# Channel sums of the nodes by way of DRAM instead of TensorE transposes, in a two-layer graph network

## The chip, the cores and the metric

The kernel runs on one core of one Trainium2 chip. The metric is the device time of one execution in microseconds (us). Three runs of the kernel before gave 2660.5 to 2662.49 us, with a median of 2661.98 us.

A core has engines with instruction streams of their own: TensorE (PE in the profile) multiplies matrices, VectorE (DVE) and ScalarE (ACT) work on elements, GpSimd (POOL) does small element work and issues DMAs, and the sync engine (SP) issues most DMAs. Each stream runs in its order; an instruction that waits for a semaphore holds back what stands behind it in its stream.

## What is computed

There are 16 graphs (B) with 1024 nodes (N) and 256 channels (C), all in float32. Both layers take relu(layernorm(x)) and add their output to x. The first layer, cut to what matters:

```python
fea = jnp.transpose(x, (0, 2, 1))            # x here is relu(layernorm(x))
c_adj = jnp.mean(fea, axis=1)                # one number for each node
diff = c_adj[:, None, :] - c_adj[:, :, None]
A = jnp.abs(jnp.abs(jax.nn.sigmoid(diff) - 0.5) - 0.5) * 2.0
Wg = adj[None, :, :] * (A + jnp.transpose(A, (0, 2, 1))) * 0.5
g = jax.nn.relu(jnp.einsum('bcn,bnm->bcm', fea, Wg) * para.reshape(1, C, N))
# q from g (4 heads of 64), k and v from x @ kv_w
attn = jax.nn.softmax(jnp.einsum('bhnd,bhmd->bhnm', q, k) * scale, axis=-1)
out = jnp.einsum('bhnm,bhmd->bhnd', attn, v)
```

The second layer multiplies by the normalized adjacency matrix, and then by two weight matrices with a batch norm after each.

The matrix A holds, for each pair of nodes, a function of the difference of their channel sums. To build 128 rows of it, the kernel needs the sums of those 128 nodes as a column (one on each partition), and the sums of all 1024 nodes as a row that is the same on every partition. The change is about how that row is made.

## The kernel before

*Layout.* A node tile has 128 nodes on the partitions; a graph has 8 of them. `Norm` computes a graph's layer norm. Its `relu` on ScalarE also sums the channels of each node into `csum`, a tile of 128 x 8: element [p, t] is the sum for node 128 t + p. That is the column form.

*The row form.* `columns_of` copies the 8 columns on VectorE, each spread over 128 elements, into two tiles `cb` of 128 x 512. `broadcast_row` transposes each of the 8 blocks of 128 x 128 on TensorE (line 199), and ScalarE copies the two PSUM banks to the tile `cbc` (line 200). `cbc` is 128 x 1024: on each partition the sums of all nodes. `differences` makes `cbc` and the generator `weigh`. The same two helpers serve the row of the degrees (`dbc`), once.

*Who reads it.* `weigh` makes the weighted matrix in 8 tiles `w`. For each, ScalarE takes two `Abs` of `cbc` with the column as bias (line 421) and a `Tanh` (line 429), and VectorE multiplies by a tile of adj (line 408) that SP has loaded (line 170).

*Order of the work.* The program order is written by hand. `attention` goes through the graphs in 16 steps each. A step issues the scores of two key tiles (line 858) and their exponentials on ScalarE (line 866), then the products with the values of the step before (line 899), and then background work until a budget is used up: `total` (lines 972 and 973) is spread evenly over the 16 steps of a graph, and each background piece yields its cost, which is added to `done`. Most pieces are products that cost 1.71.

A piece that yields `TOP` ends the step's background; what comes after it is issued in the next step right after the scores, ahead of the products with the values.

*Background of graph b* (from 1 to 13): keys and values of graph b + 1 and its queries, whose left part is the weigher's result (4 + 14 + 4 products); the second layer's `aggregate` of graph b - 1 (14 products), along which `Norm` of graph b + 2 runs; and then `prepare(b + 2, ...)`. This makes the row of graph b + 2, begins its weigher, and transposes h (`transposed`, line 379), along the 8 products of `hidden(b - 1)`, whose results ScalarE copies out as y (line 708). The products go to two PSUM banks in turn (`bank`), which `broadcast_row` and `transposed` use too. In `prepare`, one product stands ahead of `TOP` and the row, and the weigher begins after the second product.

Graph 0's row is made ahead of the attention, graph 1's at the beginning of graph 0's background, graph 2's at its end. Graphs 14 and 15 have no `prepare`, as there is no further graph.

`shifted=True` is a second version of the whole program, behind a branch that these inputs don't take.

Of the kernel before, what the change touches and what calls it, by code (L numbers as in the profile page):

```python
# [10 lines left out]
F32 = mybir.dt.float32  # L11
# [6 lines left out]
P = 128  # L18
# [5 lines left out]
def gnn_two_layers_kernel(  # L24
# [12 lines left out]
    nc = tc.nc  # L37
    B, N, C = x.shape
# [14 lines left out]
    dram = ctx.enter_context(tc.tile_pool(name="dram", bufs=1, space=DRAM))  # L53
# [15 lines left out]
    aht_d = dram.tile([7, NP // 2, P, TH, FB], F32, name="aht_d")  # L69
    y1_d = [dram.tile([P, HC, FB], F32, name=f"y1_d{i}") for i in range(B * NH)]  # L70

    sums_d = [dram.tile([2, FB], F32, name=f"sums_d{u}") for u in range(B * CC * NH)]

    UNITS = B * CC * NH
# [9 lines left out]
    def layers(shifted):  # L84
# [109 lines left out]
        def broadcast_row(dst, cbs, name):  # L194

            for g, cb in enumerate(cbs):
                pt = bank(f"cbp_{name}_{g}")
                for j in range(4):
                    nc.tensor.transpose(pt[:, j * P : (j + 1) * P], cb[:, j, :], ident)
                nc.scalar.copy(dst[:, g * FB : (g + 1) * FB], pt)  # L200
# [165 lines left out]
        TOP = -1.0  # L366
# [14 lines left out]
                    )  # L381
                nc.vector.tensor_copy(ht[:, g * FB : (g + 1) * FB], pt)

        def differences(b, cbs):

            cbcs[b] = p1.tile([P, N], F32, tag="cbc", name=f"cbc_{b}")
            broadcast_row(cbcs[b], cbs, f"c{b}")
            weighers[b] = weigh(b)

        def weigh(b):  # L390


            csum, cbc = csums[b], cbcs[b]
            made = weighted[b] = []
            adjs = []

            def load():
                q, th = divmod(len(adjs), NP)
                adjs.append(load_adj(q, th, f"adj_{b}_{q}_{th}"))

            load()
            for slot in range(2 * NH * NP + 1):
                i, odd = divmod(slot, 2)
                q, th = divmod(i, NP)
                if not odd and i > 0:

                    w, a = made[i - 1], adjs[i - 1]
                    nc.vector.scalar_tensor_tensor(w, w, 1.0, a, op0=ALU.add, op1=ALU.mult)  # L408
                    if b == 0:
                        q, th = divmod(i - 1, NP)  # L410
                        nc.vector.tensor_reduce(
                            rows[:, q, th * TH : (th + 1) * TH], a, AX.X, ALU.add
                        )
                if not odd and i < NH * NP:
                    q, th = divmod(i, NP)
                    if i + 1 < NH * NP:
                        load()
                    w = p8.tile([P, TH, FB], F32, tag="w", name=f"w_{b}_{q}_{th}")
                    made.append(w)
                    for t in range(TH):  # L420
                        nc.scalar.activation(  # L421
                            w[:, t, :],
                            cbc[:, q * FB : (q + 1) * FB],
                            AF.Abs,
                            bias=csum[:, th * TH + t : th * TH + t + 1],
                            scale=-1.0,
                        )
                if odd:
                    nc.scalar.activation(made[i], made[i], AF.Tanh, scale=-0.5 / C)  # L429
                yield 0.0  # L430
# [307 lines left out]
        def prepare(b, products):  # L738


            cbs = columns_of(csums[b], f"c{b}")
            yield from islice(products, 1)
            yield TOP
            differences(b, cbs)
            yield 1.0
            w = weighers[b]
            for k in range(CC):
                yield from weave(islice(products, 3), (0, islice(w, AHEAD // 2)))
                yield TOP
                transposed(b, k)  # L750
                yield 1.0
            yield from products
# [3 lines left out]
        def background(b):  # L756

            if b == 0:
                differences_1 = columns_of(csums[1], "c1")
                yield TOP  # L760
                differences(1, differences_1)
                yield 1.0
                for k in range(CC):
                    yield TOP
                    transposed(1, k)
                    yield 1.0
                w, products, norm = weighers[1], keys_values(1), Norm(2, True).all()
                yield from weave(
                    islice(products, 4), (0, double(islice(w, 8))), (0, islice(norm, 4))
                )  # L770
                yield from weave(
                    plain_queries(1), (0, norm), (0, w), (5, graph()), (7, degrees())
                )
                load_later()
                yield from islice(products, 1)
                cbs = columns_of(dinv, "deg")
                yield from islice(products, 1)
                yield TOP
                broadcast_row(later["dbc"], cbs, "deg")
                yield 1.0  # L780
                yield from prepare(2, products)
                return
            before = hidden(b - 1)
            gather = aggregate(b - 1)
            if b + 1 < B:
                w, products, norm = weighers[b + 1], keys_values(b + 1), normed(b - 1)
                yield from weave(islice(products, 4), (0, islice(w, 4)))
                yield from weave(queries(b + 1), (0, double(w)), (9, islice(norm, 5)))
                yield next(gather)
                yield from weave(products, (0, norm))  # L790
            else:
                yield from weave(endings.pop(), (2, normed(b - 1)))
                yield next(gather)
            if b + 2 < B:
                yield from weave(gather, (7, Norm(b + 2, True).all()))
                yield from prepare(b + 2, before)
            elif b + 2 == B:

                yield from gather
                endings.append(before)  # L800
            else:
                yield from gather
                yield from weave(before, (0, normed_last()))
# [206 lines left out]
        with st:  # L1010
            if shifted:
                for b in range(B):
                    if b > 0:
                        load_x(b)
                    run(Norm(b, True).all())
                    differences(b, columns_of(csums[b], f"c{b}"))
                    for k in range(CC):
                        transposed(b, k)
                    run(islice(weighers[b], AHEAD))
                    run(weave(plain_queries(b), (0, weighers[b])))  # L1020
                    if b == 0:
                        run(degrees(), graph())
                        load_later()
                        broadcast_row(later["dbc"], columns_of(dinv, "deg"), "deg")
                    run(keys_values(b))
                    shifted_attention(b)
                    norm = Norm(b, False)
                    run(norm.all())
                    nc.gpsimd.dma_start(out=x1_d[b], in_=xs[b])
                    if b == B - 1:  # L1030
                        attn.close()
                        turns.append(second(kind))
                    run(aggregate(b), hidden(b))
            else:
                norm = Norm(0, True)
                norm.stats(0, 1)
                norm.scale(0, 2)
                for t in range(2, NT, 2):
                    norm.stats(t, t + 1)
                    norm.shift(t - 2, 2)  # L1040
                    norm.relu(t - 2, t - 1)
                    norm.scale(t, 2)
                norm.shift(NT - 2, 2)
                norm.relu(NT - 2, NT - 1)
                products = keys_values(0)

                for k in range(CC):
                    transposed(0, k, (0,))
                run(islice(products, 2))
                for k in range(CC):  # L1050
                    transposed(0, k, (1,))
                differences(0, columns_of(csums[0], "c0"))
                run(weave(products, (0, islice(weighers[0], AHEAD))))
                load_x(1)
                load_x(2)
                run(weave(plain_queries(0), (0, weighers[0]), (5, Norm(1, True).all())))
                attention()
                attn.close()
                turns.append(second(kind))
                run(aggregate(B - 1), hidden(B - 1))  # L1060
# [324 lines left out]
```

## Time and profile before

| what | value |
|---|---|
| time, median of three | 2661.98 us |
| span of the profiled execution | 2658.7 us |
| granted TensorE clock, mean | 0.988 of full speed |
| PE busy | 2572.0 us, 97% |
| DVE busy | 1743.4 us, 66% |
| ACT busy | 1336.5 us, 50% |
| POOL busy | 564.0 us, 21% |
| transposes of line 199 for `cbc` | 128, of which 120 for graphs 1 to 15 |
| SP waiting in the adj loads of line 170 for VectorE's line 408 | 896.0 us in 71 waits |

In the views of groups, a line gives the engine, the operation, output and input tiles with their shapes, how many there are, and their durations. The timeline lists start, duration, engine and line in order of time. `SPq` is the sync engine's stream: there the duration of a merged line covers the waits between its DMAs. "DMA to landing" is the time from the issue of a transfer until its semaphore says that it is complete. A transfer that was issued behind others on the same queue includes their time.

### The profile page before, as it was taken

The numbers are of one execution on the slowest core, as the hardware profiler recorded it, in microseconds if no ns is written. First come the engines' busy times: TensorE is split into PE (matmuls) and PEld (weight loads), VectorE is DVE, ScalarE is ACT, GpSimd is POOL, SyncE is SP. The second block draws the span as 40 slices with busy tenths as digits, with TensorE's granted clock in tenths as the row PEclk, the third lists the DMA queues.
The fourth block names the chain that finished last, engine by engine and source line by source line (L and its number), as shares of the span: only waits on it lengthen the run. The fifth ranks groups of instructions, "written<-read, shape, count | busy, mean of one in ns | idle before, by whom it ended". The sixth has DMA issues, their size and how long they took to land. (4 is left out here: it accounts for less than half of the span.)

```text
span 2658.7 us, 32181 instructions
## 1 busy us (share of the span) xinstructions
PE 2572.0 (97%) x11882; PEld 951.8 (36%) x11882; DVE 1743.4 (66%) x2768; ACT 1336.5 (50%) x1937; POOL 564.0 (21%) x648
## 2 busy tenths in 40 slices
PE   8959999999999999999999999999999999999995
PEld 3323333333333333333333333333333333334443
DVE  5537576666767675767666676757676675557675
ACT  5635463636454554546373645545463634335544
POOL 1461111111111111111111111111101111026653
PEclk9989999999999999999999999999999999999997
DMA  4451424242423324242424233231524232455559
GB/s 159 145 181 61 166 80 171 84 171 80 143 92 117 122 68 158 68 171 84 171 80 156 87 131 103 93 139 60 174 80 171 80 124 99 135 198 198 198 181 374
DMA packets 131686, 355.59 MB, mean 134 GB/s; under 512 B 17984, under 2 KB 34880, under 8 KB 125376
## 3 DMA queue, kind: packets, MB, share of 16 engines
q1 hardware_dynamic: 104768, 274.25, 29.4%
q0 software_dynamic: 26752, 79.20, 9.0%
q8 instruction: 96, 1.57, 0.2%
q14 instruction: 70, 0.57, 0.1%
HBM read 278.67 MB, written 74.71 MB: 133 GB/s over the span
## 5 line engine op out<-in xcount | busy, mean ns | idle before, releaser
L866 ACT ACTIVATE p<-sc 128x1024 f32<-128x1024 f32 x512 | 495.5, 1019 | 606.3 <-PE sc L858 605.2
L888 DVE TENSOR_TENSOR acc<-acc,p 128x1024 f32<-128x1024 f32 x384 | 471.7, 1228 | 132.0 <-ACT p L866 111.5
L858 PE MATMUL sc<-q,k 64*128 64x512 f32 x2048 | 508.8, 615 | 0.5 <-ACT p L866 0.5
L899 PE MATMUL o<-p,v 128*64 128x512 f32 x2048 | 496.7, 606 | 0.0
L158 PE MATMUL pg<-w,h_a 128*64 128x512 f32 x1600 | 358.1, 592 | 3.4 <-ACT k L595 1.7
L158 PE MATMUL pa<-aht,h_b 128*64 128x512 f32 x1536 | 343.5, 592 | 0.0
L858 PEld LDWEIGHTS sc<-q,k 64*128 64x128 f32 x2048 | 176.1, 186 | 320.4 <-issue 296.8
L919 POOL DMA_DIRECT2D sums_d<-row x64 | 37.5, 586 | 1032.0 <-ACT row L918 1032.0
L158 PE MATMUL py<-at,w 128*64 128x512 f32 x1024 | 230.4, 592 | 0.0
L899 PEld LDWEIGHTS o<-p,v 128*64 128x64 f32 x2048 | 124.5, 136 | 285.4 <-issue 284.7
L408 DVE SCALAR_TENSOR_TENSOR w<-w,adj 128x1024 f32<-128x1024 f32 x128 | 157.2, 1228 | 102.9 <-ACT w L429 99.1
L158 PEld LDWEIGHTS pg<-w,h_a 128*64 128x64 f32 x1600 | 115.5, 137 | 231.8 <-issue 212.8
L158 PEld LDWEIGHTS pa<-aht,h_b 128*64 128x64 f32 x1536 | 110.4, 137 | 213.3 <-issue 197.6
L708 ACT ACTIVATE y<-py,vec 128x512 f32<-128x512 f32 x128 | 87.6, 684 | 168.2 <-PE py L158 111.4
L421 ACT ACTIVATE w<-cbc,csum 128x512 f32<-128x512 f32 x256 | 170.0, 715 | 0.0
L885 DVE TENSOR_TENSOR acc<-p,p 128x1024 f32<-128x1024 f32 x64 | 78.4, 1226 | 109.5 <-ACT p L866 109.5
L709 POOL DMA_DIRECT2D y_d<-y x128 | 70.0, 547 | 316.7 <-ACT y L708 315.6
L429 ACT ACTIVATE w<-w 128x1024 f32<-128x1024 f32 x128 | 134.9, 1054 | 1.8
L483 DVE TENSOR_TENSOR w<-w,w 128x1024 f32<-128x1024 f32 x112 | 132.8, 1216 | 1.8 <-DVE w L408 0.5
L158 PE MATMUL pv<-kvw_f,ht 128*64 128x256 f32 x1024 | 121.0, 384 | 8.8 <-DVE q L575 5.2
L924 POOL DMA_DIRECT2D inv<-sums_d x128 | 98.2, 771 | 145.8 <-DMA sums_d<-row 109.6
L158 PEld LDWEIGHTS py<-at,w 128*64 128x64 f32 x1024 | 74.2, 137 | 145.2 <-issue 128.7
(155 smaller groups left out, 2868.8 us busy)
## 6 DMA issues: line engine op xcount, KB each, us to landing
aht<-aht_d SPq DMA_DIRECT2D x224, 512.0 KB, 6.2
adj<-in_adj_dram SPq DMA_DIRECT2D x128, 512.0 KB, 4.3
y_d<-y POOLq DMA_DIRECT2D x128, 256.0 KB, 2.6
yin_f<-y_d SPq DMA_DIRECT2D x32, 1024.0 KB, 6.3
x<-in_x_dram SPq DMA_DIRECT2D x32, 512.0 KB, 5.0
para<-in_para_dram SPq DMA_DIRECT2D x64, 256.0 KB, 3.9
x_d<-x POOLq DMA_DIRECT2D x16, 1024.0 KB, 10.3
xo_f<-x_d SPq DMA_DIRECT2D x32, 512.0 KB, 8.3
```

The source lines that it names most:

```text
L158: nc.tensor.matmul(dst[r], left[:, r], right, start=start, stop=stop)
L408: nc.vector.scalar_tensor_tensor(w, w, 1.0, a, op0=ALU.add, op1=ALU.mult)
L421: nc.scalar.activation(w[:, t, :], cbc[:, q * FB : (q + 1) * FB], AF.Abs, bias=csum[:, th * TH + t : th * TH + t + 1], scale=-1.0,)
L429: nc.scalar.activation(made[i], made[i], AF.Tanh, scale=-0.5 / C)
L483: nc.vector.tensor_sub(block(i)[part], block(x)[part], block(y)[part])
L708: nc.scalar.activation(y, made, AF.Identity, bias=b1[:, j : j + 1])
L858: nc.tensor.matmul(sc[:, e, :], ks[b][k][r, m * P : (m + 1) * P], qs[b][k][r, f * FB : (f + 1) * FB], start=True, stop=True,)
L866: nc.scalar.activation(pr, sc, AF.Exp)
L885: nc.vector.tensor_add(self.acc, self.held, pr)
L888: nc.vector.tensor_add(self.acc, self.acc, pr)
L899: nc.tensor.matmul(self.o[r, :], vs[b][k][:, m, r], pr[:, e, :], start=(m == 0), stop=(m == NT - 1),)
L924: nc.gpsimd.dma_start(out=self.inv[:, :, e], in_=sums_d[u][e].rearrange("(j q) -> q j", q=P))
```

## The change

For all graphs but the first, the row no longer goes through VectorE, TensorE and ScalarE. SP writes `csum` to a DRAM row `csum_d[b]` of 1024 numbers, transposed by its addresses, and then reads this row back with a partition step of 0, so that `cbc` gets it on all 128 partitions. The second DMA waits for the first. It is meant to take the transposes from TensorE. `differences` makes the columns itself where it still needs them (graph 0). `prepare` calls it at its beginning, without a `TOP` of its own, and now two products stand ahead of the weave with the weigher, so that the weigher begins after the third product.

```diff
+    csum_d = [dram.tile([N], F32, name=f"csum_d{b}") for b in range(B)]
...
-        def differences(b, cbs):
+        def differences(b):
             cbcs[b] = p1.tile([P, N], F32, tag="cbc", name=f"cbc_{b}")
-            broadcast_row(cbcs[b], cbs, f"c{b}")
             weighers[b] = weigh(b)
+            if b == 0:
+                broadcast_row(cbcs[b], columns_of(csums[b], f"c{b}"), f"c{b}")
+                return
+            nc.sync.dma_start(out=csum_d[b].rearrange("(t p) -> p t", p=P), in_=csums[b])
+            nc.sync.dma_start(
+                out=cbcs[b], in_=csum_d[b].rearrange("(o n) -> o n", o=1).to_broadcast([P, N])
+            )
...
         def prepare(b, products):
-            cbs = columns_of(csums[b], f"c{b}")
-            yield from islice(products, 1)
-            yield TOP
-            differences(b, cbs)
-            yield 1.0
+            differences(b)
+            yield from islice(products, 2)
             w = weighers[b]
             for k in range(CC):
                 yield from weave(islice(products, 3), (0, islice(w, AHEAD // 2)))
...
             if b == 0:
-                differences_1 = columns_of(csums[1], "c1")
-                yield TOP
-                differences(1, differences_1)
-                yield 1.0
+                differences(1)
                 for k in range(CC):
                     yield TOP
                     transposed(1, k)
...
-                differences(0, columns_of(csums[0], "c0"))
+                differences(0)
                 run(weave(products, (0, islice(weighers[0], AHEAD))))
```

The calls in the shifted version change in the same way.

More of the change, by code (lines that the diff above doesn't have):

```diff
@@ L1015, in layers @@
                     run(Norm(b, True).all())
-                    differences(b, columns_of(csums[b], f"c{b}"))
+                    differences(b)
                     for k in range(CC):
```

## The prediction

> **What bounds the kernel now.** I read the page first, then the busy time by stretches, then the tile views of the row that is replaced, then the timeline of one graph's end, engine by engine.
>
> ```profile
> PE 2572.0 (97%) x11882; PEld 951.8 (36%) x11882; DVE 1743.4 (66%) x2768; ACT 1336.5 (50%) x1937; POOL 564.0 (21%) x648
> ```
>
> ```profile
> L199 PE MATMUL cbp_c<-ident,cb_c x128: 272/273/329, 18.4 to 2070.8; 128*128 128x128 f32 x128
> L200 ACT COPY cbc<-cbp_c x32: 580/592/616, 19.0 to 2071.6; 128x512 f32<-128x512 f32 x32
> ...
> 762.03:907.28 145.25, 145.05 (x699) 51.88 (x697) 98.28 (x156) 74.12 (x110) 22.10 (x30) 1.00 0.35 117
> ```
>
> The three are the page's busy times, the tile view of the row's transposes and copies (minimum, median and maximum ns) and a stretch. TensorE (PE) is busy 97% of the span. The stretch (its length, then busy us of PE, PE's weight loads, DVE, ACT and POOL, clock, DMA share, GB/s), one whole graph in the steady part (start to start of the transposes of two graphs), says it better: 145.05 us of PE in 145.25 us. So in the middle of the kernel each PE microsecond taken away is a microsecond won, and each stall put in is lost. VectorE at 98.28 us and ScalarE (ACT) at 74.12 us have room, if their work comes in time. The chain of waits covers only the end (from 2386.93 us on), and shows nothing of this change.
>
> The edge that matters is the end of a graph. PE there:
>
> ```profile
> 757.43 1.03 PE L916 MATMUL sums<-acc,ones 128*64 128x512 f32 x4
> 758.29 1.89 PE L158 MATMUL py<-at,w 128*64 128x512 f32 x8
> 760.11 1.99 PE L858 MATMUL sc<-q,k 64*128 64x512 f32 x8
> 762.02 1.09 PE L199 MATMUL cbp_c<-ident,cb_c 128*128 128x128 f32 x8
> 763.05 1.94 PE L899 MATMUL o<-p,v 128*64 128x512 f32 x8
> 764.81 5.32 PE L158 MATMUL py<-at,w 128*64 128x512 f32 x24
> 770.06 1.99 PE L858 MATMUL sc<-q,k 64*128 64x512 f32 x8
> ```
>
> and ScalarE and the sync queue (SP):
>
> ```profile
> 760.08 0.19 ACT L324 ACTIVATION_READ_ACCUMULATOR h_a<-x,lnsm_a 128x1 f32 x1
> 767.38 1.32 ACT L421 ACTIVATE w<-cbc,csum 128x512 f32<-128x512 f32 x2
> ```
>
> ```profile
> 732.34 60.55 SPq L170 DMA_DIRECT2D adj<-in_adj_dram  x6
> ```
>
> The channel sums are complete at 760.27 us, and the row `cbc` is first read at 767.38: 7.1 us. SP runs ahead: at 732.34 it had begun the adj loads of the next weigher.
>
> **What the Trainium skill says.** "TensorE: Matmul & The Clock Gate", Part 4, gives about 275 ns for one 128x128 transpose in a kernel. The trace agrees (273 ns), but they overlap: eight take 1.09 us, 136 ns each. "DMA: Bandwidth & Descriptors", Rules for kernel authors, says that a strided last dimension becomes one descriptor per element: the new write is 1024 elements of four bytes, 64 for each of 16 engines; its section Bandwidth puts such a packet at about 10.5 ns, so I estimate 0.7 us of moving. The same page (Two DMAs through the same engine are not ordered) says that the reader of what a DMA wrote has to wait on its semaphore; the two transfers are therefore a serial chain. The trace has such a pair: the `inv` gathers wait for the write to `sums_d`.
>
> **The change, part by part.**
>
> *Removed.* For 15 of 16 graphs eight transposes, two ACT copies of 0.59 us and two DVE copies of 0.42 us. On PE 15 x 1.09 = 16.4 us. ACT and DVE are not the bound; I count their 1.1 and 0.8 us per graph as nothing, hidden beside PE.
>
> *Added.* A write of 4 KB and a broadcast read of 512 KB per graph, on SP. 15 x 0.5 MB is 2% more traffic, nothing at a DMA share of 0.35. What counts is latency. For the write, the nearest rows are:
>
> ```profile
> L924 POOL DMA_DIRECT2D inv<-sums_d x128: 747/774/805, 100.7 to 2337.3; - x128
> DMA to landing us min/median/max: 2.5/2.6/5.6
> ```
>
> ```profile
> L60 SPq DMA_DIRECT2D vec<-in_vecs_dram x1: 391/391/391, 0.7 to 0.7; - x1
> DMA to landing us min/median/max: 1.6/1.6/1.6
> ```
>
> `inv` moves 512 four-byte elements in 2.6 us, `vec` 9 KB of short rows in 1.6 us. Twice as many elements as `inv`, but without GpSimd's 0.77 us of issue: bounds 2.0 and 3.5, I take 2.7. The read has the shape of an `aht` load (128 rows of 4 KB, same queue):
>
> ```profile
> L628 SPq DMA_DIRECT2D aht<-aht_d x224: 319/324/1216, 263.5 to 2354.7; - x112
> DMA to landing us min/median/max: 3.0/6.2/13.5
> ```
>
> 3.0 us alone; the median has other loads ahead in the queue, which this read doesn't have, as SP waits for the write just before it. Against it run the y stores of 256 KB. Bounds 3.0 and 7 (all 128 rows read the same 4 KB of DRAM, which no load here does); I take 3.6. With 0.2 us for two releases: 0.2 + 2.7 + 3.6 = 6.5 us (bounds 5.2 and 10.7). The row is there at 760.27 + 6.5 = 766.8.
>
> *Moved.* The budget of a step is (37.6 + 24 + 6 + 13.7) / 16 = 5.08 (lines 972 and 973), a product costs 1.71. Before `prepare` 4 + 14 + 4 + 14 products have cost 61.56. In step 12 (due 66.06) the kernel before makes one product, meets TOP and breaks; the new one makes three (66.69). So PE has, from 758.29: three products to about 763.5, scores of step 13 to 765.4, values to 767.2, two products to 770.7, scores of step 14. The first read of `cbc` on ACT stands behind the third product's y (done 764.2): ACT is there at 764.2 and waits until 766.8, some 2.6 us, 13 times (graphs 3 to 15; for graphs 1 and 2 the sums are long done).
>
> *Who is behind that wait.* On ACT: two abs (1.32), both exps of step 13 (1.94), y, tanh (1.05), y. With L the landing, exps end at L + 3.3, the two y at L + 3.95 and L + 5.7. On PE: the scores of step 14 at 770.7 need the first exp (L + 2.3) and 771.7 the second: L up to 768.3. The transposes of h at 773.2 and 773.7, behind 1.9 of scores and 0.6 of `ot`, need the two y's banks: L up to 768.0. Values of step 13 need exps at 774: not binding. So PE stalls only if the row lands after 768.0, if the chain takes over 7.7 us. My 6.5 leaves 1.2 us. On SP, behind the wait for the sums: the adj loads that now start at 732 go out after the row, about 764, and land by 769 (one 512 KB load moves in 1.7 us); the first is used behind a tanh that ends at about 771.8. Hidden beside ACT's work.
>
> *End of the graph.* Step 14 now makes three products and reaches 76.24 of a due 76.22, so step 15 has no background, and the second group of h transposes comes at the change of graph. The exps of step 15 end about 785.0 by the same count, the next scores start about 785.8: no stall. In graph 0 the removed TOP takes one of three thin attention steps away (PE waits of 0.45 and 0.47 us at 62.4 to 65.4); worth at most 1 us, not counted.
>
> Sum: 2662.0 - 16.4 = 2645.6 us.
>
> **The rivals.**
> 1. The chain is longer than the slack: the wait goes from ACT over to PE. For: two DRAM round trips, gaps of 7.1 us now, and `sums_d` to `inv` already cost POOL up to 7.3 us once. At 9.5 us the stall is 1.8 us x 13 = 23.4, less 16.4: 2669. At the upper bound of 10.7 it is 3.0 x 13 = 39, so 2684.6. Against: the queue is empty when the two go out, and quiet landings of all shapes here are 1.6 to 3.6 us.
> 2. The row lands in time, but the new order of pieces (an empty step 15, ACT's work late by 2.6 us, DVE's copies of h behind a late w) opens about 1 us per graph at PE: 13 to 16 us, which takes the gain back: 2660. For: the margins counted above are 0.8 to 1.2 us. Against: each is positive, and scores and exps are double buffered.
> 3. More is won than the transposes, as PE's first steps lose their waits and ACT and DVE are freer: 16.4 + 3 gives 2642. PE's 0.2 us of idle per graph leaves little for it.
>
> **How the numbers follow.** The forecast 0.60, rival 1 0.25 (slower in nearly all of it), rival 2 0.10 (mostly within 0.2%, 5.3 us), rival 3 0.05. So faster by over 0.2%: 0.60 + 0.05 + 0.01 = 0.66, the same 0.10, slower 0.24. The range begins at 2640, below rival 3, and reaches to 2678, a chain of 10.2 us (stall 2.5 x 13 = 32.5, less 16.4), which leaves the slow broadcast outside.
>
> **What would show it.** Right: transposes of `cbc` only in graph 0; ACT waiting some 2.6 us for the row's DMA, 13 times; the write landing near 2.7 us and the read near 3.6; a period of 144.2 us instead of 145.25, with PE busy in all but 0.2 us of it; adj loads going out after the row. Wrong: PE waiting in scores for an exp, or in h's transposes for a y, each graph; a landing after 768.0 on this clock; the period above 145.25. The step on which all hangs is the sum 2.7 + 3.6 against 7.7.

## The result and the profile after

The changed kernel takes 2772.6 us in the median (2771.43 to 2773.67), against 2661.24 us for the kernel before beside it: a ratio of 1.0418 with a 95% interval of 1.04 to 1.0436. It is 111 us slower, where 16 us less was forecast. The range given ended at 2678.

First the page of the kernel before, one line that now matters: the scores, with the number of matmuls, busy us, mean ns, and the idle time ahead of them with its releaser.

```profile
L858 PE MATMUL sc<-q,k 64*128 64x512 f32 x2048 | 508.8, 615 | 0.5 <-ACT p L866 0.5
```

The page of the kernel after (its lines of code are numbered differently: 860 is 858 before, 868 is 866, 429 is 421):

```profile
PE 2585.4 (93%) x11762; PEld 948.4 (34%) x11762; DVE 1728.3 (62%) x2738; ACT 1320.4 (48%) x1907; POOL 560.0 (20%) x648
...
L860 PE MATMUL sc<-q,k 64*128 64x512 f32 x2048 | 534.3, 642 | 105.4 <-ACT p L868 105.4
...
L429 ACT ACTIVATE w<-cbc,csum 128x512 f32<-128x512 f32 x256 | 170.4, 717 | 154.5 <-DMA cbc<-csum_d 154.5
```

TensorE (PE) was busy 97% and is busy 93%. ScalarE (ACT) now waits 154.5 us for the row's DMA, and TensorE 105.4 us for exponentials, where it waited 0.5. The scores are 25.5 us longer in sum, though they are as many as before. The loss can be read off one edge of a graph. The sync engine's timeline (start, duration; the second DMA waits for the first):

```profile
940.27 0.37 SPq L393 DMA_DIRECT2D csum_d<-csum  x1
950.93 0.32 SPq L394 DMA_DIRECT2D cbc<-csum_d  x1
```

ScalarE in the same stretch:

```profile
943.64 0.69 ACT L716 ACTIVATE y<-py,vec 128x512 f32<-128x512 f32 x1 [1.03 <-PE py L159]
956.27 1.33 ACT L429 ACTIVATE w<-cbc,csum 128x512 f32<-128x512 f32 x2 [11.95 <-DMA cbc<-csum_d]
957.51 1.91 ACT L868 ACTIVATE p<-sc 128x1024 f32<-128x1024 f32 x2
```

and TensorE:

```profile
947.20 3.60 PE L159 MATMUL py<-at,w 128*64 128x512 f32 x16
958.57 3.78 PE L860 MATMUL sc<-q,k 64*128 64x512 f32 x8 [7.76 <-ACT p L868]
```

The write is issued 0.03 us after the last sum. The read can only go out 10.66 us later. The row is first used at 956.27, 16.0 us after the write. The two exponentials of that step stand behind it on ScalarE. TensorE does the work that it still has, up to 950.8, and then waits 7.76 us for the first of them. And what follows is slow: eight matmuls of the scores take 3.78 us instead of 1.99. Why, the busy time by stretches shows (stretch, length, busy us of PE, PE's weight loads, DVE, ACT and POOL with the instructions, the granted clock, the share of the DMA engines, GB/s):

```profile
943.00:951.00 8.00, 7.81 (x36) 2.32 (x32) 0.33 (x1) 0.69 (x1) 1.78 (x4) 1.00 0.91 79
951.00:958.00 7.00, 0.00 (x0) 0.00 (x0) 0.00 (x0) 1.73 (x3) 0.00 (x0) 0.81 0.78 233
958.00:960.00 2.00, 1.44 (x4) 0.84 (x6) 1.35 (x2) 2.00 (x4) 0.00 (x0) 0.50 0.83 320
960.00:962.00 2.00, 2.00 (x6) 0.34 (x2) 2.00 (x3) 2.00 (x4) 0.72 (x2) 0.50 0.30 119
...
786.56:940.27 153.71, 146.01 (x690) 51.64 (x688) 96.99 (x154) 73.05 (x108) 22.40 (x29) 0.98 0.37 114
```

After the pause the granted clock is 0.50 for the scores. The same happens at the row of each graph from 3 to 15: 13 waits of 7.2 to 8.5 us, each with eight scores of 3.5 to 3.8 us behind it. The last line is a whole graph: 153.71 us, where it was 145.25. In the sum of this graph 7.76 of waiting, 1.79 of slow scores and 1.03 of saved transposes (see the second experiment) give +8.5 us, and 13 such graphs +111 us.

### The profile page after: what moved, and what is told of

The parts are those of the page before. It is cut to its first block, busy times and chain, and to the rows that moved or that the text cites. A ratio compares the mean times of both kernels' runs of the same rounds, so it can differ in the third digit from the quotient of the medians.

```text
span 2770.7 us, 31886 instructions
## 1 busy us (share of the span) xinstructions
PE 2585.4 (93%) x11762; PEld 948.4 (34%) x11762; DVE 1728.3 (62%) x2738; ACT 1320.4 (48%) x1907; POOL 560.0 (20%) x648
## 3 DMA queue, kind: packets, MB, share of 16 engines
q0 software_dynamic: 26752, 79.20, 11.3%
## 5 line engine op out<-in xcount | busy, mean ns | idle before, releaser
L860 PE MATMUL sc<-q,k 64*128 64x512 f32 x2048 | 534.3, 642 | 105.4 <-ACT p L868 105.4
L860 PEld LDWEIGHTS sc<-q,k 64*128 64x128 f32 x2048 | 183.4, 193 | 426.6 <-issue 279.5
L429 ACT ACTIVATE w<-cbc,csum 128x512 f32<-128x512 f32 x256 | 170.4, 717 | 154.5 <-DMA cbc<-csum_d 154.5
```

The costliest lines, as they stand in the source:

```text
L429: nc.scalar.activation(w[:, t, :], cbc[:, q * FB : (q + 1) * FB], AF.Abs, bias=csum[:, th * TH + t : th * TH + t + 1], scale=-1.0,)
L860: nc.tensor.matmul(sc[:, e, :], ks[b][k][r, m * P : (m + 1) * P], qs[b][k][r, f * FB : (f + 1) * FB], start=True, stop=True,)
```

## The experiments

All edits are against the changed kernel. Experiments 4, 8 and 12 compute what the kernel before computes. The others are made for timing alone: 1 leaves the row in another order, and the rest take it from another tensor, so that their weights are not those of the reference. "Landing" is the time from the issue of a transfer to its completion (minimum, median, maximum of 15).

**1. The same sums, written in rows of 32 bytes.**

```diff
-nc.sync.dma_start(out=csum_d[b].rearrange("(t p) -> p t", p=P), in_=csums[b])
+nc.sync.dma_start(out=csum_d[b].rearrange("(p t) -> p t", p=P), in_=csums[b])
```

> The changed kernel, but the sums are written to DRAM as they lie: 32 contiguous bytes from each partition instead of eight separate four-byte elements. The row comes out in another order (node 8p+t in the place of 128t+p), so the adjacency weights belong to wrong pairs; all work, sizes and waits are the same. Theory A (four-byte pieces in DRAM are slow to complete): the write completes in about 2.2 us instead of 8.5 to 11, the chain of both transfers takes 6 to 7.5 us, ScalarE waits 2 to 3.5 us for the row and TensorE not at all; about 2645 us, near the forecast. Rival B (any DRAM round trip at this point takes this long, whatever the pieces): the write stays above 7 us, about 2760 us or more.

Measured: 2641.23 us, a ratio of 0.992 (0.9903 to 0.9937). The sync engine's timeline:

```profile
752.57 0.32 SPq L393 DMA_DIRECT2D csum_d<-csum  x1
753.98 0.32 SPq L394 DMA_DIRECT2D cbc<-csum_d  x1
754.35 1.70 SPq L171 DMA_DIRECT2D adj<-in_adj_dram  x3
```

ScalarE:

```profile
758.85 1.33 ACT L429 ACTIVATE w<-cbc,csum 128x512 f32<-128x512 f32 x2 [2.23 <-DMA cbc<-csum_d]
```

and one graph by stretches:

```profile
608.35:752.58 144.23, 144.03 (x690) 51.02 (x688) 97.27 (x154) 73.31 (x108) 22.45 (x29) 1.00 0.37 121
```

The write is over in 1.41 us instead of 10.66, the chain takes 6.28, and TensorE runs through. The same 4 KB go the same way through DRAM: rival B falls. What took the time is the form of the write.

**2. No write, the row read from another tensor.**

```diff
-nc.sync.dma_start(out=csum_d[b].rearrange("(t p) -> p t", p=P), in_=csums[b])
...
-    out=cbcs[b], in_=csum_d[b].rearrange("(o n) -> o n", o=1).to_broadcast([P, N])
+    out=cbcs[b], in_=para[0:1, :].to_broadcast([P, N])
```

> The changed kernel without the write of the sums; the row is read from the first row of para instead, in the same broadcast and at the same place, so there is no chain and the weights are computed from another row. It shows what the removed transposes and the new order of pieces are worth without the latency. Theory A: 2643 to 2647 us, 16 below before, a period of about 144.2 us. Rival C (the new order of pieces itself leaves TensorE waiting): 2655 us or more. Under rival B the same as under A.

Measured: 2644.69 us, a ratio of 0.9933 (0.9917 to 0.995). One graph, by stretches:

```profile
583.59:727.81 144.22, 144.02 (x692) 51.01 (x688) 97.31 (x155) 73.16 (x107) 22.42 (x29) 1.00 0.37 121
```

1.03 us less than before, with TensorE idle for 0.2 us as before. So in the steady part the removed transposes are worth nearly what the timeline of the kernel before said (1.09), and the new order of the pieces costs nothing: rival C falls.

**3. The slow write kept, but nothing waits for it.** The write as in the change, the read from `para` as in experiment 2.

> The changed kernel with the slow write of four-byte elements kept, but with the row read from the first row of para (weights from another row), so that nothing waits for the write. If the loss is the wait alone (theory A): as without the write, within 3 us, 2643 to 2649 us. Rival D (the write slows the transfers beside it, the read of the row and the y stores above all): 10 us or more above the run without the write, with the read landing after 5 us or more.

Measured: 2757.58 us, a ratio of 1.0355 (1.0338 to 1.0372), nearly as slow as the change. The tile view of the row in this run, its read and how long it took to land:

```profile
L394 SPq DMA_DIRECT2D cbc<-in_para_dram x15: 566/572/574, 57.6 to 2159.7; - x15
...
DMA to landing us min/median/max: 12.1/12.6/15.0
```

and the tile view of the written row:

```profile
L393 SPq DMA_DIRECT2D csum_d<-csum x15: 370/370/462, 57.1 to 2159.3; - x15
...
DMA to landing us min/median/max: 9.9/12.1/12.6
```

The read is issued 0.4 us after the write and has no semaphore to wait for, but in all 15 cases it completes after the write, by 0.4 to 5.4 us; without the write it landed after 5.3 us (experiment 2). My theory that the loss was the dependence alone fell here: a slow write holds up the transfer behind it too. Rival D had this right.

It is not only the write's own queue. The trace of the change shows the same on GpSimd's, in the `inv` gathers (2.5, 2.6 and 5.6 us to landing in the kernel before):

```profile
L926 POOL DMA_DIRECT2D inv<-sums_d x128: 747/772/805, 99.7 to 2449.9; - x128
...
DMA to landing us min/median/max: 2.5/3.5/10.1
```

In graphs 3 to 15, 26 of them are issued while the write is under way, when the read of the row has not yet gone out. Their packets are over 2.7 to 6.9 us before the write completes, but all 26 complete only 0.2 to 2.6 us after it, 5.9 to 10.1 us after their issue.

**4. The weigher later, the transfers unchanged.**

```diff
-            yield from islice(products, 2)
-            w = weighers[b]
-            for k in range(CC):
-                yield from weave(islice(products, 3), (0, islice(w, AHEAD // 2)))
-                yield TOP
-                transposed(b, k)
-                yield 1.0
+            yield from islice(products, 5)
+            yield TOP
+            transposed(b, 0)
+            yield 1.0
+            yield from weave(islice(products, 3), (0, islice(weighers[b], AHEAD // 2)))
+            yield TOP
+            transposed(b, 1)
+            yield 1.0
...
-                yield from weave(islice(products, 4), (0, islice(w, 4)))
+                yield from weave(islice(products, 4), (0, double(islice(w, 6))))
```

> The changed kernel with the same two transfers, but the weigher begins two steps later: five products of hidden ahead of the first transposes of h, three weigher slots beside the last three products, and the slots that are left over taken two at a time in the next graph's keys (six instead of four). The chain stays as slow as it is (8.5 to 11 and 5.5 us), but it ends about when ScalarE first needs the row. Theory A: the wait of ScalarE falls from 12 us to 0 to 3, TensorE no longer waits for exps; 2645 to 2652 us. Rival C: the order costs, above 2662 us. Rival D: above 2660 us, as the stores beside the write still are slow.

Measured: 2652.99 us, a ratio of 0.9963 (0.9949 to 0.9977), just above the span that theory A gave, and better than the kernel before. One graph by stretches:

```profile
1196.58:1340.80 144.22, 144.03 (x690) 51.05 (x688) 97.42 (x154) 72.97 (x108) 22.45 (x29) 1.00 0.41 121
```

The row is still 16 to 18 us on its way, and here nobody waits for it. In the steady part the period is that of experiment 2 in most graphs, and at most 0.65 us longer (the graph after this one took 144.73), about 2 us in all. The larger part of the distance to experiment 2 lies in the first graphs: TensorE's wait in the degrees' transposes for VectorE's v copies, 4.5 us without the write, is 10.8 us here. Which transfer is held up there was not followed.

**5, 6, 7. What is slow in the write.** All with the unlinked read of experiment 3, so that only the write differs:

```diff
# 5: 64 bytes from element to element
-csum_d = [dram.tile([N], F32, name=f"csum_d{b}") for b in range(B)]
+csum_d = [dram.tile([N, 16], F32, name=f"csum_d{b}") for b in range(B)]
-nc.sync.dma_start(out=csum_d[b].rearrange("(t p) -> p t", p=P), in_=csums[b])
+nc.sync.dma_start(out=csum_d[b][:, 0].rearrange("(t p) -> p t", p=P), in_=csums[b])
# 6: half of the elements
+nc.sync.dma_start(out=csum_d[b][: N // 2].rearrange("(t p) -> p t", p=P), in_=csums[b][:, : NT // 2])
# 7: from GpSimd
+nc.gpsimd.dma_start(out=csum_d[b].rearrange("(t p) -> p t", p=P), in_=csums[b])
```

> The run with the unlinked read (row from para, weights from another row), with each of the 1024 four-byte elements written 64 bytes from the next instead of 4. As many pieces of the same size, but none in the neighbourhood of another. Theory A1 (pieces that fall into the same stretch of memory hold each other up): the write lands in 2 to 5 us instead of 12, and the time falls from 2757 to 2645 to 2665 us. Rival A2 (every small write costs its own time, wherever it goes): the write lands after 10 to 13 us as before, 2750 to 2765 us.

> The run with the unlinked read (row from para, weights from another row), with half of the elements written: the first four columns, 512 elements of four bytes, and the other half of the sums left out. If the completion grows with the number of pieces (A1 and A2 alike), the write lands after 5.5 to 7 us instead of 12 and the row comes some 5 to 6 us earlier: 2665 to 2700 us. If there is a fixed time for a write of short pieces, whatever their number (rival A3), it lands after 11 to 12.5 us, at about 2755 us.

> The run with the unlinked read (row from para, weights from another row), with the write of four-byte elements issued by GpSimd instead of SP, so that it lies in another queue than the read of the row. If the memory is what is slow (theory A): the write lands after 9 us or more from this queue too, and the read beside it, though not behind it in a queue, still takes over 5 us; 2680 to 2760 us. If it is the sync engine's queue, which serves the read only after the write (rival E): the read lands in 3 to 5 us and the time is 2645 to 2660 us.

The tile view of `csum_d` for the spread elements (2644.15 us, ratio 0.9933, 0.9913 to 0.9953):

```profile
L393 SPq DMA_DIRECT2D csum_d<-csum x15: 370/371/501, 58.0 to 2054.1; - x15
...
DMA to landing us min/median/max: 2.8/3.1/5.6
```

for half of the elements (2660.19 us, ratio 0.9993, 0.9984 to 1.0002):

```profile
L393 SPq DMA_DIRECT2D csum_d<-csum x15: 370/371/488, 53.9 to 2058.9; - x15
...
DMA to landing us min/median/max: 10.1/10.5/13.0
```

and from GpSimd (2684.23 us, ratio 1.0084, 1.0064 to 1.0104):

```profile
L393 POOL DMA_DIRECT2D csum_d<-csum x15: 899/902/1121, 57.4 to 2089.3; - x15
...
DMA to landing us min/median/max: 9.4/11.3/12.5
```

As many four-byte pieces, 64 bytes apart, land in 3.1 us instead of 12.1: rival A2 falls, and it is the neighbourhood that counts. Half as many pieces, as dense as before, still need 10.5 us: the number counts for little. A3 came nearest in this, though below its 11 to 12.5 us, and its fixed time for every write of short pieces doesn't fit the 3.1 us of the spread elements. The time of the half write says little and lies in no forecast, since this write needs only the first four node tiles' sums and goes out some 10 us earlier. From the other queue the write is as slow: it is not the sync engine's queue. The run from GpSimd didn't answer the other half of its question, as the read, no longer behind a wait for the sums, went out long before the write; the gathers under experiment 3 answer it, against rival E. What this run lost is another thing, in TensorE's waits:

```profile
PE htp L380 <- ACT y L716: 24.5, 8, 3.9
```

The y stores stand behind the write on GpSimd's queue, so their buffers come free late, and ScalarE's y and TensorE's banks after them: in this trace ScalarE's y waits 44.3 us for the y stores, in nine waits, and not at all in experiment 2.

**9, 10, 11. How dense is too dense.** As in 5, with other distances, and in 11 with each partition's elements in a stretch of its own:

```diff
# 9: [N, 2], 8 bytes apart; 10: [N, 4], 16 bytes apart
+nc.sync.dma_start(out=csum_d[b][:, 0].rearrange("(t p) -> p t", p=P), in_=csums[b])
# 11: [N, 2], 8 bytes apart, a partition's eight elements next to each other
+nc.sync.dma_start(out=csum_d[b][:, 0].rearrange("(p t) -> p t", p=P), in_=csums[b])
```

> The run with the unlinked read (row from para, weights from another row), the 1024 four-byte elements written 8 bytes apart, half as dense as in the change. The two ends are known: 4 bytes apart lands after 12.1 us in the median, 64 bytes apart after 3.1. If writes into one stretch of memory go one after another (theory A1), so that the time goes with how many share a stretch: about 3.1 + 9 x 7/15 = 7.3 us (6 to 8.5). If only direct neighbours disturb each other (rival A4), so that any gap is enough: 3 to 4 us.

> The same with the elements 16 bytes apart. Theory A1: 3.1 + 9 x 3/15 = 4.9 us to landing (4.2 to 6). Rival A4: 3 to 4 us.

> The run with the unlinked read (row from para, weights from another row), elements 8 bytes apart, but in the order of the partitions: the eight elements of one partition lie in one stretch of 64 bytes, and no other partition writes there. As dense as the run with 8 bytes[...]. If it is several engines at once that hold each other up (A5): 3 to 4 us to landing. If it is the number of writes to a stretch, whoever sends them (A1): as with 8 bytes, 6 to 8.5 us.

One execution each. The landings of the write, in the order 9, 10 and 11:

```profile
DMA to landing us min/median/max: 4.1/4.6/8.1
```

```profile
DMA to landing us min/median/max: 3.0/3.4/5.6
```

```profile
DMA to landing us min/median/max: 5.9/6.3/8.2
```

| distance of the four-byte elements | landing, median us | device time, us |
|---|---|---|
| 4 bytes (experiment 3) | 12.1 | 2757.6 |
| 8 bytes | 4.6 | 2662.8 |
| 8 bytes, a partition's own stretch | 6.3 | 2686.4 |
| 16 bytes | 3.4 | 2648.8 |
| 64 bytes (experiment 5) | 3.1 | 2644.2 |

A1 in its simple form, a time that goes with the number in a stretch, asked for 7.3 and 4.9 us at 8 and 16 bytes and got 4.6 and 3.4; A4 was nearer, but 8 bytes aren't quite free. A5 asked for 3 to 4 us where a partition's pieces lie together, and it falls as far as such pieces come from one DMA engine, which these traces don't show: they are slower (6.3) than those of neighbouring partitions at the same distance (4.6), where A1 asked for the same. Whether the time goes by in the memory or on the way to it is not settled.

**8, 12. Versions that beat both kernels.** Experiment 1 left the row in another order. The reader can put it right:

```diff
+            order = "r (c p) -> r c p" if b == 0 else "r (p c) -> r c p"
+            nodes = cbc.rearrange(order, p=P)
...
                         nc.scalar.activation(
-                            w[:, t, :],
-                            cbc[:, q * FB : (q + 1) * FB],
+                            w[:, t, :].rearrange("r (c p) -> r c p", p=P),
+                            nodes[:, q * FB // P : (q + 1) * FB // P, :],
```

> Rows of 32 contiguous bytes written as in the run of that layout, and the row's order put right where it is read: for all graphs but the first, ScalarE reads cbc with a step of eight elements (node 128t+p lies at 8p+t), so the weights are those of the reference again. If a step of 32 bytes costs ScalarE nothing: Abs stays at about 0.71 us, 2640 to 2643 us, 0.8% below before. If strided reads are slower, Abs takes 1.4 us, 16 of them add 11 us of ScalarE per graph, which has 70 us free: 2641 to 2655 us.

Measured: 2645.67 us, a ratio of 0.9935 (0.9919 to 0.9952). The tile view of the row (count, then minimum, median and maximum ns):

```profile
L431 ACT ACTIVATE w<-cbc,csum x256: 705/1232/1296, 23.6 to 2110.8; 128x512 f32<-128x512 f32 x128
```

The strided Abs takes 1.23 us instead of 0.71. In the steady part that is hidden; what is lost against experiment 1 is lost in the first graphs. The last version takes graph 1 out; the rest is as in 8:

```diff
-            nc.sync.dma_start(out=csum_d[b].rearrange("(t p) -> p t", p=P), in_=csums[b])
+            layout = "(t p) -> p t" if b == 1 else "(p t) -> p t"
+            nc.sync.dma_start(out=csum_d[b].rearrange(layout, p=P), in_=csums[b])
...
+            order = "r (c p) -> r c p" if b < 2 else "r (p c) -> r c p"
```

> The version with contiguous 32-byte rows and ScalarE's strided reads, but graph 1, whose row is needed 18 us after its sums, by the slow write in the right order, so that its Abs run at 0.71 us instead of 1.23 in the crowded first graphs. If these strided reads are what the strided version lost in the first 320 us against the run with the permuted row (5 us): 2641 to 2644 us. If the slow write disturbs that stage as much: 2645 to 2650 us.

Measured: 2641.35 us, a ratio of 0.993 (0.9913 to 0.9946): the lowest median of a version with the weights of the reference. The intervals of the last two versions overlap; the medians, which differ by 4.3 us, suggest that the strided reads of graph 1 were the difference, but this is not shown.

## Why the prediction was wrong

*The step that failed* is "Twice as many elements as `inv`, but without GpSimd's 0.77 us of issue: bounds 2.0 and 3.5, I take 2.7". In graphs 3 to 15 the write took 8.5 to 11.1 us between its issue and that of the read, three to four times the value and at least 2.4 times the upper bound. The row chosen to bound it was the wrong one: `inv` reads four-byte pieces from DRAM, and the change writes them there, side by side. No transfer in the trace of the kernel before does that, so the trace had nothing that bounded it from above. The estimate of the moving was good (0.7 us; the packet records of the change have 1024 pieces within 0.64 us). What follows the last piece, 7 to 9.5 us until the completion, was not in it. The Trainium skill, "DMA: Bandwidth & Descriptors", Anatomy of one DMA, says for the path from GpSimd that the semaphore comes only when the last byte is confirmed in the target memory, and that this is most of the fixed time of a DMA, about 2 us. The runs agree in the place, not in the size: the dense write took 11.3 us from GpSimd and 12.1 from the sync engine, and only rows of 32 bytes (1.4) and pieces 16 or 64 bytes apart (3.4 and 3.1) are near 2.

*The read*, 3.6 us in the sum, was mis-sized too: it landed after 5.6 us in the median in the change, and in experiment 1 the row was used 4.9 us after the read's issue. With a write of 2.7 us, the 5.6 would have made a chain of 8.5 us, 0.8 over the slack; by the prediction's formula that costs some 10 us and leaves the change faster than the kernel before. With the 1.4 us that the write of experiment 1 took, there was room for it.

*The slack of 7.7 us was right, to within 0.6.* "The scores of step 14 need the first exp (L + 2.3)": with the first use of the row at 956.27 that gives 958.57, which is when they start. A chain of 16.0 and a wait of 7.76 leave 8.2. With a chain of 6.3 us (experiment 1) TensorE doesn't wait, as the working said.

*Rival 1 was the case that came, with a bound too low.* It ended at a chain of 10.7 us and 2684.6. Its own formula with the measured 16.0 us gives 13 x 8.3 - 16.4 = +92 us. The remaining 20 us are in the main a term that the prediction didn't have: the clock. After a pause of 7.76 us the scores run at 0.50 and take 1.79 us more, 13 times: 23 us. (Summed from the trace, 100 us of waits and 23 of slow scores, less 13.4 of transposes, make 110 of the 111.) The Trainium skill, "TensorE: Matmul & The Clock Gate", Part 1, gives the half clock after an idle window of about 3.4 us. These traces agree: 0.50 after 7.76, while in experiment 11, with waits of 1.3 to 2.3 us at this place, eight scores took 2.0 to 2.6 us.

*The other steps held.* The transposes were worth 1.03 us per graph (1.09 in the forecast). That the kernel without the write gained 17.4 us in all, near the 16.4 of the forecast, is partly luck: 13.4 of it are the steady part, the rest came from outside it. The order of the pieces cost nothing (rival 2). The copies taken from ScalarE and VectorE gave nothing measurable in the steady part. The adj loads did go out after the row, and nobody waited for them in experiment 1 beyond one wait of 4.0 us, which the kernel before has too (3.9). The first graphs gave more than the "at most 1 us" there: of the 20.9 us of experiment 1, 13 x 1.03 = 13.4 are the steady part, and the transposes of graphs 1 and 2 are some 2 of the rest.

## What to carry to other kernels

A DMA that scatters single float32 values side by side into DRAM can't be priced by its bytes or by the time in which its pieces move, and hardly by their number. What costs is its completion, and a row of the trace that moves the other way doesn't bound it. It can also hold up what other queues have under way. Write what each partition has as one run, and pay for the order where it is cheap: here in the reader's access pattern. When a wait is put on an engine that isn't the bottleneck, work out for how long the bottleneck can live on what is already queued, and add the slow clock if it can't.

## What the runs showed that was not expected

- 1024 elements of four bytes next to each other in DRAM complete after 8.4 to 12.6 us, 512 after 10.5 in the median, the same 1024 in rows of 32 bytes after 1.4, and at 64 bytes of distance after 3.1.
- A read that is independent of such a write, but issued behind it on the same queue, landed after 12.6 us in the median. Gathers on GpSimd's queue that were issued during the write completed only after it, 5.9 to 10.1 us after their issue.
- ScalarE's Abs over 128 x 512 with a step of 32 bytes between the elements read took 1.23 us, against 0.71 for adjacent ones.
